# A four-stream graph-attention kernel: one more row by transfer, independent scatters, and a new interleaving of the streams

## The chip, the cores and the metric

The kernel runs on one core of a Trainium2 chip. The metric is the device time of one execution in microseconds (us); times of a kernel are medians of several runs. Engines are called PE (TensorE), DVE (VectorE), ACT (ScalarE), POOL (GpSimd) and SP (SyncE, which here only issues transfers).

## What is computed

The input x has 32 batches of 512 nodes with 256 features, in float32, and one adjacency of 512 x 512. Four layers follow each other. Each normalizes x over the features, takes the positive part h, computes a graph attention and adds the result to x:

```python
h = jnp.maximum(_layernorm(x, axis=-1), 0.0)
x = x + layer(h, adj, W, a)
# an attention: Wh = h @ W; s_i = Wh @ a1; s_j = Wh @ a2
# e = leaky_relu(s_i[:, :, None] + s_j[:, None, :]); masked by adj
# out = softmax(e) @ Wh, then elu or relu
```

Layers 0 and 1 have one head. Layer 2 has four heads of 64 features. Layer 3 is a linear layer to 512 features, an attention without a mask, a second linear layer to 256, and a masked attention, with residuals.

## The kernel before, in words

**An attention without exponentials of a matrix.** With exp taken of each node's two terms alone, exp(leaky_relu(s_i + s_j)) becomes a factor times max(r_i, t_j). So the 512 x 512 weights of a head are one DVE operation per tile of 128 rows: max of a row r, spread over all partitions, with a column t, times the mask (`weights`, L698, its operation at L708). The row r comes in one of two ways. On PE: four transposes of a column that is broadcast to 128 columns fill a PSUM bank (L704, through the helper at L425). By transfers: `rows_out` (L715) makes one small transpose and one store of rows to DRAM, and `spread` (L725) reads one row back to all 128 partitions, 256 KB, into one of three buffers. Layers 0, 1 and the last attention use PE. In layer 2 (L805) heads 1 to 3 use transfers and head 0 uses PE (L822). The products of layer 2 use 32-column tiles of the array, 16 to a bank (`beside`, L419).

**The unmasked attention by sorting.** `sort_attend` (L949) replaces a 512 x 512 product: it spreads one row of terms, counts for each node its place in the order (L969), and POOL scatters the rows of values to DRAM by that place: two orders (halves of the features) of four tiles each, one indirect transfer a tile (L990). SP reads an order back in sequence (L997, L998). DVE and PE make prefix sums from both sides: DVE within a partition (L1008 to L1017), PE across partitions with triangular matrices (`add_up`, L895, called `before` and `after`). SP writes the sums as a table (L1031), and POOL gathers for each node its row of the table (L1039, two buffers). DVE and ACT finish a gathered tile (L1053 to L1058), and `mlp_in` (L1105) turns it by four transposes on PE. Only the last batch uses the direct product (`attend`, L917).

**Four streams and a list scheduler.** Four streams of eight batches each are written as generators. Each `yield` returns a time on a notional clock at which the stream wants to go on (`after_us`, L411, from PE work issued times STRETCH and a given number of us times SLOW). The loop at L1152 always resumes the stream with the earliest time. So the yields set the order in which operations are written down, and nothing else: they are no waits on the chip. That order is each operation's rank. A planner in the kernel's own file (`price`, `jobs_of`, `in_order`) then places all operations on the engines: at each step the operation of the lowest rank whose inputs are ready on its own cost table, with PSUM banks and buffers given out. `LANDING` (L79) and L126 are its assumed times from issue to landing of transfers; `holds` is how long an issue keeps an engine. `arrange` (L376) fixes the order found, engine by engine. Waits on the chip remain real semaphores. SP, POOL, DVE and ACT run strictly in that order, so what stands behind a waiting instruction waits too.

**PSUM banks.** There are eight; each stream has a tag, and a tag's tiles may take one bank of its own or any of four shared ones. `bank` (L430) gives a tile the tag of the stream whose turn it is, and, while other streams haven't started or have ended, their tags in turn.

**Setup.** Weights, adjacency and x are loaded on SP. The mask comes from the adjacency by one DVE comparison (L563), one POOL operation (L564) and 16 transposes on PE with four copies on ACT (L575). Other weights get their attention columns by small products (`project`, L466). The setup is a fifth generator, resumed every 4.0 us of the notional clock from 7.5 on.

Of the kernel before, what the change touches and what calls it, by code (L numbers as in the profile page):

```python
# [78 lines left out]
LANDING = {"sums": 5600.0, "spread": 4400.0, "table": 6500.0, "x": 10000.0, "order": 4100.0, "g": 6300.0, "out": 4500.0}  # L79
# [26 lines left out]
def price(job, outs, ins, in_psum):  # L106
# [15 lines left out]
    if op == "DMACopy":  # L122
        name, _, s = outs[0]
        kind = name.split("_")[0].rstrip("0123456789")
        large = elements(s) * s[0][1] > 5000
        job.took = LANDING.get(kind, 5000.0) if large else 5200.0 if kind == "table" else 2250.0  # L126
        job.holds = (2000.0 if kind == "order" else 1290.0) if e == "Pool" else 600.0 if kind in ("sums", "table") else 400.0
        return
# [28 lines left out]
def jobs_of(instructions, homes):  # L157

    jobs, users, seen, pitch = [], {}, {}, {}
    for place, ins in enumerate(instructions):  # L160
# [6 lines left out]
        for write, access in [(False, a) for a in reads] + [(True, a) for a in writes]:  # L167
# [16 lines left out]
            kept = []  # L184
            for other, wrote, b in seen.get(name, []):
                meets = b[0] < box[1] and box[0] < b[1] and any(c < y and x < d for c, d in b[2] for x, y in box[2])
                if meets and (write or wrote) and other is not job:
                    job.real.add(other)
                    if write and on_chip and box[0] <= b[0] and b[1] <= box[1] and len(box[2]) == 1 and box[2][0][0] <= b[2][0][0] and b[2][-1][1] <= box[2][0][1]:
                        continue  # L190
                kept.append((other, wrote, b))
# [184 lines left out]
def arrange(tc, order):  # L376

    instructions = real_instructions(tc)
    edge = mybir.DependencyInfo(mybir.DependencyClass.NoSync, mybir.DependencyReason.DATA)
    for line in order.values():  # L380
        for a, b in zip(line, line[1:]):
            tc.add_manual_dep(instructions[b], instructions[a].name, edge, reason="arranged")
# [3 lines left out]
def fast(ctx, tc, plan, flag, x, adj, w0, a0, w1, a1, w2, a2, mlp1_w, mlp1_b, mlp2_w, mlp2_b,  # L386
# [10 lines left out]
    LEAD = 75.0  # L397
    SLOW = 1.5
    STRETCH = 2.0
# [27 lines left out]
    active = set()  # L427
    banks = [0]

    def bank():  # L430

        own = [turn[0], *(i for i in range(NS) if i not in active and i != turn[0])]
        banks[0] += 1
        return psum.tile([P, N], FP, tag=f"b{own[banks[0] % len(own)]}", name="b", bufs=8 // NS)
# [125 lines left out]
    def setup():  # L560
# [9 lines left out]
        for j in range(NT):  # L570
            turn[0] = NS - 1 - j % (NS - 1)
            p = bank()
            for t in range(NT):
                transpose(p[:, t * P:(t + 1) * P], own[:, t, j * P:(j + 1) * P], ident)
            nc.scalar.copy(maskT[:, j, :], p)  # L575
        turn[0] = NS - 1
# [70 lines left out]
    def turned(xn, when):  # L647
# [5 lines left out]
        yield after_us(0.6)  # L653
# [9 lines left out]
    def values(hT, w, rs=None):  # L663

        v = work.tile([P, NT, F + 3], FP, tag="v", name="v", bufs=4)
        for t in range(NT):
# [14 lines left out]
            if t + 1 < NT:  # L681
                yield after_us(0)
        yield after_us(0.8)
        return v

    def linear_t(inT, w, bias, name, bufs):
# [3 lines left out]
        for f in range(ft):  # L690
# [4 lines left out]
            yield after_us(0.9 if f == ft - 1 else 0)  # L695
# [47 lines left out]
    def plain(hT, w, rs=None):  # L743
# [3 lines left out]
        yield after_us(3.2)  # L747
# [19 lines left out]
    def layer0(xt, xn, rs, when):  # L767
        v, wt = yield from plain((yield from turned(xn, when)), W0)
        xn, rs = new_xn(), small([NT], "rs")
        for t0 in range(0, NT, 2):  # L770
            r, q = pair(), pair("q")
            for i in range(2):
# [3 lines left out]
                if i == 0:  # L776
                    yield after_us(0)
            add_elu(xt[:, t0:t0 + 2, :], r, q)
            norm(xt, xn, rs, t0, True)
            last, when = when, after_us(6)  # L780
            if t0 == 0:
                yield after_us(0)
# [3 lines left out]
    def layer1(xt, xn, rs, when):  # L786
        v, wt = yield from plain((yield from turned(xn, when)), W1, rs)
        xn, rs = new_xn(), small([NT], "rs")
        for t0 in range(0, NT, 2):
            r = pair()  # L790
            for i in range(2):
                p, rd = averages(v, wt, t0 + i)
                nc.scalar.activation(r[:, i, :], p, AF.Relu, scale=rd)
                if i == 0:
                    yield after_us(0)
# [3 lines left out]
            last, when = when, after_us(5)  # L799
            if t0 == 0:  # L800
                yield after_us(0)
# [3 lines left out]
    def layer2(xt, xn, rs, when):  # L805
        hT = yield from turned(xn, when)
        v = work.tile([P, NT, NH, CH], FP, tag="v", name="v2", bufs=4)
        for t in range(NT):
# [11 lines left out]
            yield after_us(0 if t + 1 < NT else 1)  # L820
        row_d = rows_out(v[:, :, :, D + 2], NH)
        far = [spread(row_d[h, :]) if h else None for h in range(NH)]  # L822
        wts = []

        def begin():
# [4 lines left out]
            return after_us(3.2)  # L830
# [6 lines left out]
        )  # L837
        begin()
        note(v.rearrange("p t h c -> p (t h) c")[:, :, D:])
        yield after_us(3)  # L840
        when = begin()
        for g, parts in enumerate(plan):
# [10 lines left out]
            yield after_us(0.9)  # L853
# [29 lines left out]
            yield after_us(0)  # L883
# [3 lines left out]
        yield after_us(7)  # L887
        return xn, rs, after_us(2)
# [28 lines left out]
    def attend(oT, b):  # L917

        halves, ends = fc_values()
        for c in range(2):  # L920
            for t in range(NT):
                project_half(oT, halves, ends, c, t)
                yield after_us(0)
# [4 lines left out]
        yield after_us(2)  # L928
        ys = []
        for t in range(NT):  # L930
# [10 lines left out]
            yield after_us(0)  # L941
            if t:
                mlp_in(oT, ys[t - 1], t - 1)
                yield after_us(0)
        yield after_us(3)
        mlp_in(oT, ys[-1], NT - 1)
        yield after_us(1)

    def sort_attend(oT, b):  # L949
# [6 lines left out]
        for t in range(NT):  # L956
            project_half(oT, halves, ends, 0, t)
            yield after_us(0)
        project_half(oT, halves, ends, 1, 0)
        yield after_us(0)  # L960
# [3 lines left out]
        yield after_us(7.0)  # L964
# [10 lines left out]
        sort = after_us(6)  # L975
        yield after_us(0)
        for t in range(1, NT):
            project_half(oT, halves, ends, 1, t)
            yield after_us(0)
# [7 lines left out]
        for c in range(2):  # L987
            yield sort
            for t in range(NT):
                nc.gpsimd.indirect_dma_start(  # L990
                    out=orders[c], out_offset=bass.IndirectOffsetOnAxis(ap=at[:, 0, t:t + 1], axis=0),
                    in_=halves[c][:, t, :], in_offset=None,
                )
            flat.append(work.tile([P, NT * 2, C], FP, tag="sums", name="sums", bufs=2))
            u = flat[c].rearrange("p (t k) n -> p t k n", k=2)[:, :, 1, :]
            rows = orders[c].rearrange("(p t) c -> p t c", t=NT)
            nc.sync.dma_start(u, rows)  # L997
            nc.sync.dma_start(flat[c][:, 2, :], rows[:, 0, :])  # L998
            sort = after_us(2)
        places = table[:N, :].rearrange("(p t) (k c n) -> p (t k) c n", t=NT, k=2, c=2)  # L1000
        sort = after_us(11)
        for c in range(2):
# [15 lines left out]
            yield after_us(3)  # L1018
# [14 lines left out]
            sort = after_us(1)  # L1033
        yield after_us(9)
# [12 lines left out]
        landed = after_us(6)  # L1047
        for t in range(NT):
# [13 lines left out]
            landed = after_us(3)  # L1062
            when.append(after_us(4))
# [6 lines left out]
        yield after_us(1.0)  # L1070

    def layer3(xt, xn, when, b):
# [6 lines left out]
        for t0 in range(0, NT, n):  # L1079
            y, q = pair()[:, :n, :], pair("q")[:, :n, :]  # L1080
            for i in range(n):
# [3 lines left out]
                yield after_us(0)  # L1085
# [40 lines left out]
    def batch(b):  # L1126
        if b < NS:
            first_norm(b)
            yield after_us(4)
        else:  # L1130
            yield after_us(4)
        xt, xn, rs = normed.pop(b)
        when = after_us(2)
# [14 lines left out]
    ready = {i: i * LEAD for i in range(NS)}  # L1148
    streams = [stream(i) for i in range(NS)]
    early = setup()  # L1150
    ready[NS] = 7.5
    while ready:  # L1152
        i = min(ready, key=ready.get)
        if i == NS:
            turn[0] = NS - 1
            ready[i] += 4.0
# [5 lines left out]
        active.add(i)  # L1162
        wait = next(streams[i], None)
        if wait is None:
            del ready[i]
            active.remove(i)
# [456 lines left out]
```

## Time and profile before

| | us |
|---|---|
| median of 3 runs | 2814.35 |
| lowest, highest | 2813.93, 2819.74 |
| the profiled execution, own time | 2815.09 |
| its span in the trace | 2812.3 |
| PE busy | 2754.0 |
| DVE busy | 2255.0 |
| ACT busy | 1615.8 |
| POOL busy | 513.7 |

The mean granted clock of PE is 0.996 of full speed. 278.98 MB moved, at a mean of 99 GB/s; the 16 transfer engines are busy for some three tenths. All numbers of the profile are from one execution. The page has busy shares of each engine and of 40 slices of the span, the groups of instructions with their mean durations and what ended the idle time before them, and the transfers. Other views answer for a window: busy time by stage, who waited for whom, and a timeline. In them PE is the matmul row and PEld the weight load, which overlaps it; SPq is SP's queue.

### The profile page before, as it was taken

How to read it: one execution, taken by the hardware profiler on the slowest of the kernel's cores; microseconds unless marked ns; L12 is line 12 of the kernel's file. 1: busy time of each engine (PE TensorE's matmuls, PEld its weight loads, DVE VectorE, ACT ScalarE, POOL GpSimd, SP SyncE). 2: the span in 40 equal slices, each digit the busy share in tenths (PEclk: the TensorE clock that was granted, in tenths of full speed). 3: DMA queues.
4: the chain of work that ended last, by engine and by line, in shares of the span. 5: the costliest groups of instructions: out<-in, count | busy, mean ns of one | idle time of the engine just before them, and what ended most of it. 6: DMA issues, size and time to landing. Idle time of an engine off the chain costs nothing.

```text
span 2812.3 us, 41762 instructions
## 1 busy us (share of the span) xinstructions
PE 2754.0 (98%) x14444; PEld 1969.4 (70%) x14444; DVE 2255.0 (80%) x5834; ACT 1615.8 (57%) x4142; POOL 513.7 (18%) x515
## 2 busy tenths in 40 slices
PE   6999999999999999999999999999999999999987
PEld 5667677767767776767766677776676767777665
DVE  4778887887869879788887888878888788878854
ACT  3446656566556566566665565655655556565544
POOL 0011121122211212122111122011220212211220
PEclk9999999999999999999999999999999999999999
DMA  3023332333323333243331433223332332323320
GB/s 98 23 93 104 107 110 83 103 109 114 109 92 97 119 113 101 71 124 107 117 114 42 121 125 119 93 84 100 119 110 91 106 114 96 109 85 104 109 98 33
DMA packets 197890, 278.98 MB, mean 99 GB/s; under 512 B 17644, under 2 KB 156838, under 8 KB 197672
## 3 DMA queue, kind: packets, MB, share of 16 engines
q1 hardware_dynamic: 167912, 177.95, 20.4%
q0 software_dynamic: 29760, 98.30, 10.4%
q8 instruction: 115, 1.88, 0.3%
q14 instruction: 103, 0.84, 0.1%
HBM read 160.75 MB, written 115.45 MB: 98 GB/s over the span
## 4 chain that ended last, share of the span: by engine, by line
PE 81%; DVE 13%; DMA 3%; ACT 3%; issue 1%; POOL 0%; SPq 0%; ACTq 0%; DVEq 0%; POOLq 0%
PE b L417 62%; PE b L421 10%; PE b L425 9%; DVE w L708 4%; DVE st L624 2%; DMA spread<-row 1%; DVE y L765 1%; DVE y L1094 1%; DMA row<-row 1%; DVE y L758 1%; DVE xn L635 1%; DVE x L759 1%; DMA g<-table,at 0%; DVE q L763 0%; DVE x L797 0%
## 5 line engine op out<-in xcount | busy, mean ns | idle before, releaser
L417 PE MATMUL b<-v,w 128*128 128x257 f32 x3136 | 739.9, 382 | 7.3 <-DVE w L708 7.3
L417 PEld LDWEIGHTS b<-v,w 128*128 128x128 f32 x3136 | 580.9, 191 | 118.8 <-issue 28.6
L417 PE MATMUL b<-WFC,oT 128*128 128x256 f32 (+1 forms) x2048 | 490.4, 380 | 0.0
L417 PEld LDWEIGHTS b<-WFC,oT 128*128 128x128 f32 x2048 | 375.6, 189 | 56.4 <-issue 7.2
L417 PE MATMUL b<-W,hT 128*128 128x259 f32 (+1 forms) x1536 | 389.7, 387 | 1.5 <-ACT hT L645 1.5
L990 POOL DMA_INDIRECT order<-v,at x248 | 269.7, 1087 | 498.3 <-ACT y L852 163.9
L708 DVE SCALAR_TENSOR_TENSOR w<-b,v,maskT 128x512 f32<-128x512 f32 x512 | 353.3, 744 | 3.6 <-PE b L425 3.5
L421 PE MATMUL b<-w,v 128*32 128x512 f32 x3072 | 349.5, 595 | 0.0
L417 PEld LDWEIGHTS b<-W,hT 128*128 128x128 f32 x1536 | 276.0, 191 | 79.3 <-issue 25.3
L1039 POOL DMA_INDIRECT g<-table,at x124 | 125.6, 1013 | 1116.4 <-DVE q L763 251.3
L708 DVE SCALAR_TENSOR_TENSOR w<-spread,v,maskT 128x512 f32<-128x512 f32 x384 | 286.0, 786 | 28.1 <-DMA spread<-row 25.3
L417 PE MATMUL b<-hT,WM 128*128 128x512 f32 x512 | 241.5, 594 | 2.3 <-ACT hT L645 2.2
L421 PEld LDWEIGHTS b<-w,v 128*32 128x32 f32 x3072 | 89.9, 110 | 205.9 <-issue 205.9
L417 PE MATMUL b<-oT,WM 128*128 128x512 f32 x512 | 232.3, 600 | 0.8 <-DVE oT L1112 0.8
L624 DVE BATCH_NORM_STATS2 st<-x 128x6 f32<-128x256 f32 x512 | 195.1, 409 | 2.1
L765 DVE TENSOR_TENSOR y<-q,y 128x512 f32<-128x512 f32 (+1 forms) x194 | 132.3, 682 | 63.9 <-ACT q L764 59.3
L417 PEld LDWEIGHTS b<-oT,WM 128*128 128x128 f32 x512 | 96.6, 191 | 107.0 <-issue 96.6
L425 PEld LDWEIGHTS b<-ident,xn 128*128 128x128 f32 x1024 | 121.3, 141 | 64.3 <-issue 25.4
L425 PE MATMUL b<-ident,xn 128*128 128x128 f32 x1024 | 152.8, 276 | 7.8 <-DVE xn L635 2.7
L645 ACT ACTIVATE hT<-b 128x512 f32<-128x512 f32 x256 | 149.5, 595 | 14.2 <-PE b L425 14.2
L740 DVE RECIPROCAL rden<-b 128x1 f32<-128x1 f32 x388 | 58.4, 158 | 120.3 <-PE b L417 119.6
L915 ACT ACTIVATE v<-b,ends 128x256 f32<-128x256 f32 x256 | 120.0, 470 | 58.3 <-PE b L417 52.4
(154 smaller groups left out, 4230.1 us busy)
## 6 DMA issues: line engine op xcount, KB each, us to landing
table<-sums SPq DMA_DIRECT2D x62, 1032.0 KB
spread<-row SPq DMA_DIRECT2D x127, 256.0 KB
sums<-order SPq DMA_DIRECT2D x62, 516.0 KB
x<-in_x_dram SPq DMA_DIRECT2D x32, 512.0 KB
out_dram<-x SPq DMA_DIRECT2D x62, 256.0 KB
sums<-order SPq DMA_DIRECT2D x62, 129.0 KB
order<-v,at POOLq DMA_INDIRECT x248, 2.7
g<-table,at POOLq DMA_INDIRECT x124, 5.3
```

Source lines behind the costliest of these rows:

```text
L417: nc.tensor.matmul(p, w, x, **flags)
L421: nc.tensor.matmul(p, w, x, tile_position=(0, c), **flags)
L425: nc.tensor.transpose(p, x, i)
L624: nc.vector.bn_stats(st[:, i, :], xt[:, t0 + i, :])
L635: nc.vector.tensor_scalar(xn[:, t0 + i, :], xt[:, t0 + i, :], mv[:, i, 0:1], rp[:, i:i + 1], op0=OP.subtract, op1=OP.mult)
L645: nc.scalar.activation(hT[:, :, t0 * P:(t0 + 2) * P], p.rearrange("p (k n) -> p k n", k=KF), AF.Relu)
L708: nc.vector.scalar_tensor_tensor(wt[:, j, :], r, t_col(j), maskT[:, j, :], op0=OP.max, op1=OP.mult)
L740: nc.vector.reciprocal(r, den)
L765: nc.vector.tensor_tensor(r, q, r, op=OP.add)
L915: nc.scalar.activation(halves[c][:, t, :F], ps[:, :F], AF.Copy, scale=ends[:, t, 0:1])
L990: nc.gpsimd.indirect_dma_start(out=orders[c], out_offset=bass.IndirectOffsetOnAxis(ap=at[:, 0, t:t + 1], axis=0), in_=halves[c][:, t, :], ...
L1039: nc.gpsimd.indirect_dma_start(out=g, out_offset=None, in_=table, in_offset=bass.IndirectOffsetOnAxis(ap=at[:, 1, t:t + 1], axis=0),)
```

## The change

It has five parts.

1. **Head 0 by transfer.** In layer 2 all four rows come by `spread`. The first weights are written down 9.98 notional us after the rows' stores.
2. **Independent scatters.** The four scatters of one order are declared to be free of each other, since they write different rows; both reads of the order get explicit waits on all four. The planner no longer orders them among themselves either. On POOL, `arrange` adds order edges to the next five instructions in place of the next one.
3. **Assumed landing times.** `spread` 4300 ns plus 900 for each later head (4400), gathers 6800 (6300), row stores 2600 and small others 3300 (2250), the first x 5000 (10000), the adjacency 9000 (5000).
4. **Yields.** Nearly all numbers of `after_us` change, LEAD goes from 75.0 to 75.63 with an offset for each stream, SLOW from 1.5 to 1.43, STRETCH from 2.0 to 1.5. The setup is resumed every 1.5 us from 0.35 on.
5. **Banks.** A tile always takes the tag of its own stream; the mask's transposes no longer walk through other streams' tags.

In the order of instructions the changed program has 384 transposes of v on PE where there were 512, 512 products with a spread row and 384 with a row in PSUM (384 and 512), and 159 spread transfers (127). All other counts are the same.

```diff
-LANDING = {"sums": 5600.0, "spread": 4400.0, "table": 6500.0, "x": 10000.0, "order": 4100.0, "g": 6300.0, "out": 4500.0}
+LANDING = {
+    "sums": 5600.0, "spread": 4300.0, "table": 6500.0, "x": 10000.0, "order": 4100.0, "g": 6800.0, "out": 4500.0,
+    "adj": 9000.0,
+}
+SHORT = {"table": 5200.0, "row": 2600.0, "out": 4500.0}
...
-        job.took = LANDING.get(kind, 5000.0) if large else 5200.0 if kind == "table" else 2250.0
+        job.took = LANDING.get(kind, 6000.0) if large else SHORT.get(kind, 3300.0)
+        if kind == "spread":
+            job.took += 900.0 * (ins[0][1] // 512)
+        if kind == "x" and ins[0][1] == 0:
+            job.took = 5000.0
...
+            free = write and name in apart
             for other, wrote, b in seen.get(name, []):
+                if free and wrote and b == box:
+                    kept.append((other, wrote, b))
+                    continue
...
-    for line in order.values():
-        for a, b in zip(line, line[1:]):
-            tc.add_manual_dep(instructions[b], instructions[a].name, edge, reason="arranged")
+    for e, line in order.items():
+        for reach in range(1, 6 if e == "Pool" else 2):
+            for a, b in zip(line, line[reach:]):
+                tc.add_manual_dep(instructions[b], instructions[a].name, edge, reason="arranged")
...
-    LEAD = 75.0
-    SLOW = 1.5
-    STRETCH = 2.0
+    LEAD = 75.63
+    SLOW = 1.43
+    STRETCH = 1.5
...
-        own = [turn[0], *(i for i in range(NS) if i not in active and i != turn[0])]
-        banks[0] += 1
-        return psum.tile([P, N], FP, tag=f"b{own[banks[0] % len(own)]}", name="b", bufs=8 // NS)
+        return psum.tile([P, N], FP, tag=f"b{turn[0]}", name="b", bufs=8 // NS)
...
-        far = [spread(row_d[h, :]) if h else None for h in range(NH)]
+        far = [spread(row_d[h, :]) for h in range(NH)]
...
-            return after_us(3.2)
+            return after_us(1.36)
...
+        yield after_us(9.98)
         begin()
         note(v.rearrange("p t h c -> p (t h) c")[:, :, D:])
-        yield after_us(3)
+        yield after_us(7.5)
...
-        yield after_us(7)
-        return xn, rs, after_us(2)
+        yield after_us(9.4)
+        return xn, rs, after_us(1.32)
...
-        yield after_us(7.0)
+        yield after_us(0.73)
...
-        sort = after_us(6)
-        yield after_us(0)
+        sort = after_us(16.48)
+        yield after_us(7.62)
...
+            placed = []
             for t in range(NT):
-                nc.gpsimd.indirect_dma_start(
+                one = nc.gpsimd.indirect_dma_start(
                     out=orders[c], out_offset=bass.IndirectOffsetOnAxis(ap=at[:, 0, t:t + 1], axis=0),
                     in_=halves[c][:, t, :], in_offset=None,
                 )
+                for other in placed:
+                    tc.declare_no_dep(one.ins, other.ins, reason="rows of one order apart")
+                placed.append(one)
...
-            nc.sync.dma_start(u, rows)
-            nc.sync.dma_start(flat[c][:, 2, :], rows[:, 0, :])
-            sort = after_us(2)
+            landed = mybir.DependencyInfo(mybir.DependencyClass.Sync, mybir.DependencyReason.DATA)
+            for read in (nc.sync.dma_start(u, rows), nc.sync.dma_start(flat[c][:, 2, :], rows[:, 0, :])):
+                for other in placed:
+                    tc.add_manual_dep(read.ins, other.ins.name, landed, reason="rows of four tiles")
+            sort = after_us(1.66)
...
-        sort = after_us(11)
+        sort = after_us(6.05)
...
-        yield after_us(9)
+        yield after_us(4.72)
...
-    ready = {i: i * LEAD for i in range(NS)}
+    ready = {i: i * LEAD + late for i, late in enumerate((0, -2.47, -0.73, -8.03))}
...
-    ready[NS] = 7.5
+    ready[NS] = 0.35
...
-            ready[i] += 4.0
+            ready[i] += 1.5
```

The other yields change in the same way, in every layer: those within a loop over tiles from 0 to between 0.06 and 12.63, those between stages up or down by a few us.

## The prediction

> **What bounds the kernel now.** I read the page's busy shares and slices first, then busy time by stage, then the groups by shape, then who waited for whom on PE and in the queues, and at last the timeline of both ends.
>
> ```profile
> PE 2754.0 (98%) x14444; PEld 1969.4 (70%) x14444; DVE 2255.0 (80%) x5834; ACT 1615.8 (57%) x4142; POOL 513.7 (18%) x515
> PE   6999999999999999999999999999999999999987
> ```
>
> PE is busy all along and short only in the first slice and the last two. The span, 2812.3, is 2754.0 of PE plus 58.3 of idle. The stages (columns: stage, its length, then busy us and instructions of PE, weight loads, DVE, ACT, POOL; granted clock; DMA share; GB/s) say where those 58.3 lie:
>
> ```profile
> 0.00:6.90 6.90, 0.02 (x1) 0.05 (x1) 0.63 (x4) 1.28 (x1) 1.14 (x8) 1.00 0.55 167
> 6.90:17.50 10.60, 2.90 (x12) 2.44 (x12) 5.30 (x6) 0.74 (x2) 2.27 (x3) 1.00 0.86 263
> 17.50:33.50 16.00, 13.75 (x68) 11.46 (x68) 5.13 (x22) 7.56 (x21) 0.84 (x4) 1.00 0.67 181
> 33.50:73.60 40.10, 35.61 (x197) 29.82 (x198) 23.98 (x82) 18.63 (x54) 1.47 (x3) 1.00 0.00 1
> ...
> 1000.00:2000.00 1000.00, 997.07 (x5262) 715.35 (x5261) 830.51 (x2151) 589.47 (x1520) 189.34 (x184) 1.00 0.33 104
> ...
> 2680.00:2700.00 20.00, 16.69 (x59) 9.23 (x56) 11.07 (x31) 12.24 (x29) 7.41 (x8) 0.91 0.38 120
> 2706.00:2718.00 12.00, 7.61 (x22) 4.92 (x21) 9.97 (x19) 2.30 (x7) 0.00 (x0) 0.64 0.25 88
> ...
> 2741.00:2757.00 16.00, 10.55 (x46) 8.25 (x45) 9.73 (x20) 10.44 (x20) 1.59 (x2) 0.79 0.25 83
> ```
>
> The first 214.9 us hold 27.7 of idle, 220 to 2500 only 6.6, the rest 24.7, of which 8.8 follow the last matmul that counts. Between the ends the kernel runs at the rate of PE: only PE work taken out shortens it there. At the ends it is bound by chains that too few streams cover.
>
> **PE work.** Each of 32 batches loses the four transposes that spread head 0's row (L704 by L425).
>
> ```profile
> L425 PE MATMUL b<-ident,v 128*128 128x128 f32 x512 | 83.7, 274 | 1.4 <-ACT v L675 0.8 <-ACT v L674 0.3 <-ACT v L677 0.2
> ```
>
> Its pace is seen in PE's timeline (start, length, line, tiles, count):
>
> ```profile
> 2730.20 0.60 PE L425 MATMUL b<-ident,ends 128*128 128x128 f32 x4
> 2730.70 3.74 PE L417 MATMUL b<-v,w 128*128 128x257 f32 x16
> ```
>
> A mean of 274 ns is latency. In the timeline four such take 0.60 to the end of the last, which itself lasts 0.27, so they start (0.60-0.27)/3 = 110 ns apart; the median start-to-start of this group is 109. 128 x 109 ns = 14.0. The upper bound is the group's busy share, 83.7/512 = 163 ns, or 20.9; the following matmul comes 0.50 after the first of four, so I take 14.0. The order of instructions, before against after, shows nothing else gone from PE: as many matmuls of each other shape, and 193 changes between tile modes in both. **-14.0.**
>
> **What comes in for it.** 32 more transfers of 256 KB on SP's queue, 8.4 MB on 279 (3%), and 32 x 0.35 = 11 us of SP's issue time. Head 0's four products now read SBUF: the two groups of L708 have means of 744 (from PSUM) and 786 ns, so 128 x 42 ns = 5.4 us on DVE, 0.2 points on 80%. Both lie beside PE. On the path is only the row's trip. In the first batch the 16-row transpose is at 73.6, the first product at 80.8, and four take 2.7: some 10 us to the last. I priced PE's new order with start-to-start distances of the trace (109 ns a transpose; 217, 219, 226 and 429 for one pass of 257, 259, 268 and 512 columns, two passes each; 310 a prefix matmul). Between that transpose and the first use of head 0 lie 18.4 to 23.2 us of other PE work, 13.1 in the first batch: hidden. If it were not, 3 us late 32 times is 96 us. Only three spread buffers exist, so the fourth transfer waits on SP for head 0's last product; behind it stand another stream's row, its spread and reads of orders. Bounds for that: 0 (head 3's first use comes 10.4 us or more after head 0's, and its trip and products need 7), and 1 us a batch on PE, nearest to the row "DVE w L708 <- DMA spread<-row: 25.3, 16, 2.9", which costs PE nothing now. I take 0.
>
> **The scatters.** On POOL the eight scatters of a batch alternate now between two orders, and start within 12 us (12.7 to 24.3 after the row's transpose in the first batch), though one holds POOL 0.98.
>
> ```profile
> POOL order L990 <- DMA order<-v,at: 43.6, 48, 2.6
> ```
>
> and in SP's own queue:
>
> ```profile
> SPq L997 <- DMA order<-v,at: 658.9, 54, 27.3
> ```
>
> 43.6 us of waits on landings go. In the new POOL order each order's four stand together, so the first order's last issue moves from the seventh place to the fourth: 6 us earlier or more. SP, which stands 658.9 us at L997 with table writes and spreads behind it, is free earlier. No matmul waits for this now, so it is worth 0 by itself; it pays for the next item.
>
> **The new order in the middle.** Changed yields cost nothing on the chip: they set ranks. They shorten what covers the sort. In PE work, from the ends' row transpose to the first transpose of a gathered tile there are 81.7 to 86.1 us before, 70.6, 70.9, 71.9 and 78.6 after; from the second order's last prefix matmul to that transpose 25 to 31 before, 20.8 to 23.9 after. What the chain needs there is seen where it had no cover, in the drain: prefix to table issue 1.7, table to the gathered product 13.1 to 14.3, product to transposes 4.6: 19.4 to 20.6. It fits by 0.3 to 4. Bounds: 0, and 1 us for three batches in four, 23. It planned with the same holds and longer landings for gathers (6.8 for 6.3; the trace's median is 5.3, largest 7.6), so I take little: **+3.**
>
> **The start.** PE's idle comes from one wait and then many.
>
> ```profile
> PE b L425 <- POOL own L564: 7.7, 1, 7.7
> PE b L417 <- DVE w L708: 5.1, 5, 2.0
> ```
>
> The new DVE order puts x's statistics first (now at 19.4, behind copies that wait for loads), but the mask's first step (L563, at 9.5 now) behind the copy of the four-head weights, which ends at 17.8. Then 1.2 on DVE, 1.9 on POOL: the mask's transposes start at 21.0, not 17.5. Meanwhile x's transposes and two products are done. On DVE the first weights stand behind the tie band, whose mask waits on POOL behind the last weights' load (28.0): 28.4 + 0.9 + 0.6 + four small ones, so 30.6, not 32.8. First averages near 31.4 instead of 33.5: -2. After that PE's order holds stream 1's layer 0 from 29 us of work on (before 39) and stream 2's from 57 (before 82): more to fill with. Idle from 33.5 to 214.9 is 10.9; I halve it, bounds 0 and -9. **-7.**
>
> **The drain.** From 2664 to 2804 PE idles 15.6 us, and the clock is granted at 0.64 to 0.97 in places: weighted by PE's busy time some 7 more. The Trainium skill ("TensorE: Matmul & The Clock Gate", section "Part 1: The HAM clock gate") halves the clock only after an idle window of about 3.4 us. In 2706:2718 no idle stretch exceeds 1.2 us and the clock is 0.64. By the page only the idle could come back; by the row each short stall in a thin stretch costs about half as much again. I go by the row. In the new order batch 30's prefix matmuls alternate with batch 31's first linear layer and batch 29's averages (before, few others stand there: 4.4 idle); the last gathered tile of batch 29 has 33.6 us since its prefix, and needs about 31 (2.9 idle now); batch 30's gathers have covers of 18.6, 24.2 and 25.9 against needs of 19.4, 27 and 29: 4.2 idle for 5.5. Of 22.7 some 13 stay. Bounds -1 and -16. **-9.** The tail of 8.4 us behind the last average is the same code: 0.
>
> **Sum.** 2812.3 - 14.0 + 3 - 7 - 9 = 2785.3 span. The profiled execution took 2815.09, 2.8 beyond its span, and lies 0.7 above the median 2814.35: so 2787.
>
> **Rivals.**
> 1. *Only the transposes count.* The ends stay, as each end's chain is latency whichever stream fills: -14 + 3 gives 2803. For it: the mask is later by 3.5. Against it: two and three streams stand side by side on PE much earlier. 0.23.
> 2. *The ends close almost wholly*: -14 - 12 - 16, and nothing lost between, 2772. Against it: the gathers' cover in the drain is still short. 0.10.
> 3. *The sort falls behind its shorter cover*, at the gathered tiles' transposes (L1108 by L425), in every steady batch. If DVE or SP takes the table 3 us later than in the drain, three batches in four stall 2 to 3 us: 23 x 2.5 = 58 less 30, 2842. It decides from about 1.3 us a batch (30/23). For it: the margin is 0.3 to 4 and SP carries more. Against it: the scatters give 6 us to the front, and DVE has 17% idle. 0.08.
> 4. *It doesn't do what it says*: the scatters still wait, the fourth spread holds SP, and the shift eats most of the gain: 2812. 0.05.
>
> The forecast itself has 0.54. 0.2%, 5.6 us, is about what a measurement can tell from no change: below 2808.7 is faster, above 2820 slower. Faster 0.86, within 0.06, slower 0.08. Range 2771 to 2807: it takes in both rivals on the fast side and the bounds of start and drain, and leaves out the slow two.
>
> **What would show it.** Right: PE near 2733 to 2740 busy; 384 transposes of v; 512 products from spread near 0.75 us; idle under 10 between 220 and 2500; POOL with no waits of order on order; the mask's transposes near 21 and first averages near 31; the clock at 1.00 in more of the drain. Wrong: PE waits for L765 or for spread in each period of 340 us; a first slice as empty as before; SP waiting at L728 for products.

## The result and the profile after

The changed kernel takes 2784.09 us (median of 4 runs, 2782.5 to 2786.01), beside 2814.63 for the kernel before on the same chip: ratio 0.9888, 95% interval 0.9871 to 0.9905. The forecast was 2787. The profiled execution took 2783.36, with a span of 2781.5, 30.8 less than before. The sum came out right, in part by luck: three of its terms are 6 to 8 us off, and the misses partly cancel.

PE's busy time and its row of slices, from the page of the changed kernel:

```profile
PE 2740.6 (99%) x14316; PEld 1953.5 (70%) x14316; DVE 2272.9 (82%) x5834; ACT 1636.1 (59%) x4142; POOL 518.1 (19%) x515
PE   7999999999999999999999999999999999999998
```

PE is busy for 13.4 us less, 0.6 above the forecast's 2733 to 2740, and the last two slices are nearly full. The first slice holds hardly more than before (7 tenths for 6). The stages, columns as in the prediction:

```profile
6.90:17.50 10.60, 6.76 (x24) 4.83 (x23) 4.18 (x14) 3.37 (x10) 0.49 (x3) 1.00 0.85 261
17.50:33.50 16.00, 11.36 (x55) 10.25 (x56) 6.46 (x16) 5.62 (x14) 3.55 (x6) 0.92 0.68 181
33.50:73.60 40.10, 34.91 (x184) 30.30 (x183) 19.32 (x64) 16.66 (x47) 0.00 (x0) 0.86 0.00 1
...
1000.00:2000.00 1000.00, 999.52 (x5248) 709.56 (x5247) 845.64 (x2164) 603.23 (x1527) 195.43 (x191) 1.00 0.34 108
...
2700.00:2720.00 20.00, 17.42 (x85) 14.55 (x83) 8.79 (x19) 9.67 (x20) 5.22 (x6) 1.00 0.51 170
2720.00:2740.00 20.00, 18.03 (x66) 12.23 (x67) 8.82 (x20) 10.34 (x21) 0.00 (x0) 0.91 0.01 4
```

The middle has 0.5 us of idle in 1000 (2.9 before). The drain has its clock back (0.91 in the worse of these two stages, 0.64 before). At the start the column falls from 1.00 to 0.92 and 0.86. But its 1.00 there is no full clock: the records of the clock begin only at 26.4 us before and at 24.2 us after, and where there is no record the column counts 1, and so does the mean of 0.996 for the kernel before. PE's timeline of the kernel before shows the pace there:

```profile
17.54 2.83 PE L425 MATMUL b<-ident,own 128*128 128x128 f32 x12 [7.66 <-POOL own L564]
```

These transposes start 214 ns apart, in the prediction's lines from the drain 109. The changed kernel's start 214 apart too. So both kernels run at half clock up to the first record, with PE busy for 10.2 us before and 11.8 after. What the changed kernel has besides is half clock from 31.0 to 37.9, from 51.5 to 58.4 and from 89.1 to 92.5. Who waited on PE, and in SP's queue:

```profile
PE b L438 <- DVE xn L637: 8.2, 11, 3.8
...
PE b L438 <- POOL own L572: 4.3, 1, 4.3
PE b L438 <- DVE y L771: 3.5, 3, 1.6
```

```profile
SPq L1009 <- DMA order<-v,at: 696.9, 92, 17.7
...
SPq L734 <- DVE w L714: 4.0, 1, 4.0
```

No product of layer 2 stands for a spread's landing. On SP a spread stood once, for 4.0 us, behind a product (L734 issues spreads), so head 0's row came at no cost. The wait of POOL's scatters on each other's landing is gone. SP's waits for the scatters to land (L1009) did not shrink in sum, but SP stands there earlier: the first order's read leaves 6.7 us after the first scatter (median of 31 batches), 12.7 before, and the first gather 43.9 us after it, 48.3 before.

One row needs care, since the experiments turn on it. L771 (L765 before; the line shifts by a few in the variants) is the last DVE step of `elu2_plus1`, and its only result that PE transposes is a finished gathered tile (in `mlp_in`), save in the last batch, where it ends the direct product. So PE's wait on this `y`, anywhere but in the drain, is a wait for gathered rows. The changed kernel has three, all in the drain.

**Where the 30.8 us lie.** I priced each kernel's PE order as the prediction did (start-to-start distances of the trace), scaled it by 1.0042, with which the changed kernel's middle comes out without loss, and compared that with the times in the trace. What a stretch takes beyond its price is lost there, be it idle time or half clock. The start ends at the row transpose (of `ends`) of the fifth sorted batch, the middle at that of the 29th, the drain with the last matmul. "PE work" is the price of the whole order. The first matmul and the tail take 15 us in both.

| | PE work | lost at the start | in the middle | in the drain |
|---|---|---|---|---|
| before | 2735.5 | 32.9 | 2.9 | 25.9 |
| after | 2721.5 | 33.8 | -0.2 | 11.0 |
| difference | -14.0 | +0.9 | -3.1 | -14.9 |
| forecast | -14 | -7 | +3 | -9 |

How a loss is split between start and drain depends on these prices to within some 3 us.

### The profile page after: what moved, and what is told of

It is laid out like the page before. It is cut to its first block, busy times and chain, and to the rows that moved or that the text cites. A ratio compares the mean times of both kernels' runs of the same rounds, so it can differ in the third digit from the quotient of the medians.

```text
span 2781.5 us, 41668 instructions
## 1 busy us (share of the span) xinstructions
PE 2740.6 (99%) x14316; PEld 1953.5 (70%) x14316; DVE 2272.9 (82%) x5834; ACT 1636.1 (59%) x4142; POOL 518.1 (19%) x515
## 4 chain that ended last, share of the span: by engine, by line
PE 94%; DVE 3%; ACT 1%; DMA 1%; issue 0%; SPq 0%
PE b L430 72%; PE b L434 12%; PE b L438 10%; DVE st L630 0%; DMA W<-in_L_gnn_W_dram 0%; DVE xn L637 0%; DVE y L771 0%; DVE y L764 0%; DVE y L1107 0%; DVE w L714 0%; DMA WHA<-in_L_gnn_W_hand_dram 0%; DMA row<-row 0%; ACT q L780 0%; DMA x<-in_x_dram 0%; ACT y L1097 0%
## 5 line engine op out<-in xcount | busy, mean ns | idle before, releaser
L430 PE MATMUL b<-v,w 128*128 128x257 f32 (+1 forms) x3136 | 767.1, 382 | 2.0 <-DVE w L718 1.0
L430 PEld LDWEIGHTS b<-v,w 128*128 128x128 f32 x3136 | 573.5, 191 | 122.8 <-issue 34.2
L430 PE MATMUL b<-W,hT 128*128 128x259 f32 (+1 forms) x1536 | 396.4, 388 | 0.5 <-ACT hT L651 0.5
L714 DVE SCALAR_TENSOR_TENSOR w<-spread,v,maskT 128x512 f32<-128x512 f32 x512 | 373.9, 778 | 13.7 <-PE b L434 13.1
L998 POOL DMA_INDIRECT order<-v,at x248 | 262.4, 1058 | 409.1 <-DVE at L980 147.0
L714 DVE SCALAR_TENSOR_TENSOR w<-b,v,maskT 128x512 f32<-128x512 f32 x384 | 264.5, 741 | 21.9 <-PE b L438 19.7
L1110 POOL TENSOR_TENSOR x<-x,y 128x512 f32<-128x512 f32 x62 | 82.6, 1332 | 1038.2 <-ACT y L1108 1029.0
L1052 POOL DMA_INDIRECT g<-table,at x124 | 134.9, 1088 | 563.1 <-DMA table<-sums 267.3
L771 DVE TENSOR_TENSOR y<-q,y 128x512 f32<-128x512 f32 (+1 forms) x194 | 132.2, 682 | 33.6 <-ACT q L770 33.4
L922 ACT ACTIVATE v<-b,ends 128x256 f32<-128x256 f32 x256 | 120.6, 471 | 64.0 <-PE b L430 51.5
```

The lines of the kernel that those rows point to most:

```text
L430: nc.tensor.matmul(p, w, x, **flags)
L714: nc.vector.scalar_tensor_tensor(wt[:, j, :], r, t_col(j), maskT[:, j, :], op0=OP.max, op1=OP.mult)
L771: nc.vector.tensor_tensor(r, q, r, op=OP.add)
L922: nc.scalar.activation(halves[c][:, t, :F], ps[:, :F], AF.Copy, scale=ends[:, t, 0:1])
L998: one = nc.gpsimd.indirect_dma_start(out=orders[c], out_offset=bass.IndirectOffsetOnAxis(ap=at[:, 0, t:t + 1], axis=0), in_=halves[c][:, t ...
L1052: nc.gpsimd.indirect_dma_start(out=g, out_offset=None, in_=table, in_offset=bass.IndirectOffsetOnAxis(ap=at[:, 1, t:t + 1], axis=0),)
```

## Experiments

**The theory and its rivals.** My theory was that of the prediction's sum: each term stands for itself, so that the transposes alone are worth 14 us, the yields alone the ends, and the scatters about nothing. The first rival was that parts need each other. From the second set of runs on there was another: the planner draws a new plan at each edit, and it is the plan that costs. Each kernel's time is given with its ratio to the kernel before on the same chip; the changed kernel stands at 0.9888, which would be 2786 on the chips of these runs, where the kernel before took 2817.5 to 2817.7. The losses are those of the table above.

**1. The transfer alone**, on the kernel before:

```diff
-        far = [spread(row_d[h, :]) if h else None for h in range(NH)]
+        far = [spread(row_d[h, :]) for h in range(NH)]
```

> The kernel before with one edit: head 0's row by the transfer too. 128 transposes (109.4 ns each) leave TensorE: 14.0 us. Theory A (each cause adds up: the transposes are worth 14.0 and nothing waits for the row): 2800 us, ratio 0.9950, with the start, the middle and the drain losing what they lose in the kernel before (32.9, 2.9 and 25.9 us). Rival (in the order of before, whose first batch of head 0 work stands only a few us behind the row, the trip of the row is not hidden): TensorE waits for the spread in each batch, 1 to 3 us x 32, 2810 to 2840 us.

2880.79 us, ratio 1.0227 (1.0209 to 1.0245): 63 slower with 14.0 us of work less. The rival's mechanism is right, and its size too small. Lost: 56.6 at the start, 65.7 in the middle, 19.2 in the drain. The waits on PE, for the first weights and for the gathered tiles:

```profile
PE b L417 <- DVE w L708: 43.0, 26, 7.8
PE b L425 <- DVE y L765: 17.8, 12, 2.9
```

In this plan 11.0 to 15.9 us of PE work lie over the row's trip, and PE stands for the first weights. Then comes something that I had not priced. Once in each period of four batches (some 341 us) the waits crowd together, and the clock falls to half for 3.4 to 6.8 us behind them.

**2. The yields alone**, on the kernel before: LEAD, SLOW, STRETCH, all numbers of `after_us`, the streams' starts and the setup's ranks as in the change, the wait of 9.98 among them. POOL's longer order edges and the explicit waits of the reads stayed in too; the rest is as before.

> The kernel before with only the new yields, LEAD, SLOW, STRETCH, stream starts and setup ranks; 512 transposes, chained scatters, old landing times, old banks. Theory A (the interleaving alone made the gain beyond the transposes, 14.9 us in the drain, 3.1 in the middle, -0.9 at the start): 2797 us, ratio 0.994. Rival B (the yields were set for independent scatters and revised landing times, and without those the sort chain or the drain stalls): 2815 to 2845 us, with TensorE waiting for the gathered rows or the order's reads in the middle.

2852.35 us, ratio 1.0123 (1.0106 to 1.0139). My theory fell here too. Lost: 47.0, 30.6, 22.2. The rival is right, in its waits too; only its range ended 7 us lower. The longest row on PE is that of the gathered tiles:

```profile
PE b L430 <- DVE y L770: 25.5, 29, 4.8
```

10.7 us of it, in 21 waits, lie in the middle, where the kernel before has 1.5 in 4. The chain of work behind one of them begins at the gather (start, length, what):

```profile
1059.07 7.14 DMA g<-table,at
...
1066.23 0.76 DVE g L1063
...
1068.80 0.61 DVE y L770
...
1069.46 0.77 PE b L430 x5
```

The gather takes 7.1 us from issue to landing, and the tile's transposes stand for it.

**3. The changed kernel with head 0's row by PE again** (the first diff, turned round).

> The changed kernel with head 0's row by TensorE again (512 transposes), all else kept. Theory A (terms add up): +14.0 us, 2798 us. Rival (the new yields hold room for the transfer's trip, which is now left empty of nothing, and the row's arrival was costing something): less than +12 us, 2793 to 2796. If the transposes' place moves the ends too: outside 2793 to 2803.

2820.86 us, ratio 1.001 (1.0001 to 1.0019), some 35 slower than the changed kernel. 14.0 are work; the rest is lost at the start (40.4) and in the middle (16.9); the drain is not worse (9.4). The sum holds for the work and fails for the rest.

**4. Room for the row on the kernel before.** Experiment 1 and one wait more:

```diff
+        yield after_us(9.98)
         begin()
         note(v.rearrange("p t h c -> p (t h) c")[:, :, D:])
```

> The kernel before with head 0's row by the transfer and one wait more: 9.98 us between the rows' transfers and the first head's weights, as the change has it. In TensorE's order 20.0 to 27.3 us of work now lie between the rows' transposes and the first product of head 0 (11.0 to 15.9 with the transfer alone, 18.4 to 23.2 in the changed kernel). Theory A (the transfer alone lost time because the row's trip of some 18 us was not covered; with cover it is worth its 14 us): the waits for L708's weights are gone and the time is 2800 us. Rival (the other waits that appeared with the transfer, for results of DVE and ScalarE in stages far from the row, are from an order that no longer fits its yields, and one wait doesn't mend them): waits for L708 gone, but 2820 to 2850 us.

2860.55 us, ratio 1.0153 (1.0139 to 1.0166). The rival is right in kind; its range ended 10 us lower. The row's waits nearly go, and other stages stall:

```profile
PE b L417 <- ACT hT L645: 17.3, 32, 0.9
...
PE b L417 <- DVE w L708: 4.9, 6, 1.3
```

Lost: 46.8, 46.9, 29.8. L645 is the copy of a transposed h, far from layer 2's rows.

**5. The changed kernel without that wait.**

```diff
-        yield after_us(9.98)
         begin()
```

> The changed kernel without the one wait of 9.98 us between the rows' transfers and the first head's weights. TensorE's order then has 11.4, 16.8, 17.2 and 13.8 us of work over the row's trip in place of 18.4 to 23.2. Theory A (that wait is what hides the trip): TensorE waits for the spread's weights in the middle, 1 to 3 us a batch, and the time is 2825 to 2850 us. Rival (the trip is hidden by the work of the other streams wherever the wait stands): 2784 to 2790 us.

2955.39 us, ratio 1.0492 (1.0478 to 1.0507). Theory A has the right sign; the size, some 170 us, is about three times what I expected, 145.1 in the middle alone. In this plan DVE stands for the spread's landing, and PE behind it, also in other streams' work:

```profile
DVE w L714 <- DMA spread<-row: 51.1, 9, 7.5
```

```profile
PE b L430 <- DVE w L714: 32.8, 23, 1.8
PE b L434 <- DVE y L874: 21.4, 7, 3.1
PE b L438 <- ACT y L1096: 18.6, 7, 2.7
PE b L438 <- DVE y L771: 17.2, 10, 2.6
```

Experiments 1, 4 and 5 together show: without the wait the trip is not hidden, and with it nearly so. The 18 to 23 us over the row are made by this one wait among the new yields, not by the transfer.

**6. Transfer and yields together**, on the kernel before: experiments 1 and 2 in one; chained scatters, old landing times and old banks.

> The kernel before with the transfer and the new yields together, without the three other parts: scatters chained, old landing times, old choice of PSUM banks. Theory A (the pair is the change; each of the two alone lost time because it needs the other, and the three other parts are worth a few us at most): 2784 to 2792 us. Rival B (independent scatters and the revised landing times are what lets the sort's shorter cover hold, and the banks what lets the start hold): 2800 to 2840 us, with waits for the gathered rows in the middle or a start that loses over 40 us.

2815.94 us, ratio 0.9998 (0.9989 to 1.0007). Rival B holds, by the second of its signs: the start loses over 40. Lost: 42.7, 12.7, 21.7. Gathered tiles hardly stop PE in the middle (2.8 us at L770). So the pair alone gains nothing, 31 us short of the whole change.

**7. The scatters chained, and the planner told so.**

```diff
-            free = write and name in apart
+            free = False
...
-                for other in placed:
-                    tc.declare_no_dep(one.ins, other.ins, reason="rows of one order apart")
```

> The changed kernel with each order's four scatters chained again; the rest kept. In the changed kernel the eight scatters of a sorted batch take some 10 us, 1.3 us apart; chained they took 13 to 14. The cover from the last prefix product to the first use of a gathered row becomes 19.9 to 22.7 us (20.7 to 23.9 before the edit). Theory A (the chain of the sort has slack in the middle, so the scatters are worth little): within 4 us of the changed kernel, 2784 to 2788. Rival (my prediction's claim that independent scatters pay for the shorter cover): TensorE waits for gathered rows, 0.5 to 1.5 us a batch in 24 batches, 2796 to 2820.

2838.83 us, ratio 1.0085 (1.0071 to 1.0099). The rival is right in sign and too small (40.8 are lost in the middle), and it names only a part of the waits. In the middle PE stands 11.6 us for gathered tiles, at their transposes (L771) and at the step behind those (`oT` of L1123), and 7.5 for `oT` of L700, which is another stage. The chain of work between 1299 and 1310 shows how a late sort gets there (start, length, what):

```profile
1299.90 0.41 DVE sums L1026
1300.31 0.18 SPq L1042
...
1300.54 0.02 SPq L734
...
1300.58 6.42 DMA spread<-row
...
1307.03 1.63 DVE w L714
```

One stream's table write (L1042) stands at the head of SP's queue until DVE has its sums; behind it stands another stream's spread (L734), which lands 6.4 us later, and only then come that stream's weights. This is one place of several. The chain reaches `oT` of L700 at 1309.62, and PE stands for it.

**8. The scatters chained on the chip, but not in the plan.** Only the last two removed lines of experiment 7; the planner goes on as if they were free.

> The changed kernel in which the planner still counts an order's four scatters as independent, but the program doesn't declare them so: on the chip each waits for the one before. TensorE's planned order stays that of the changed kernel almost line for line. Theory A (the 55 us that chained scatters cost together with a new plan come from the scatters themselves: the order is read some 4 us later, the table is written later, SP stands on that write and a spread behind it is late): 2820 to 2845 us. Rival B (they come mostly from the new plan): 2785 to 2800 us.

2827.5 us, ratio 1.0031 (1.0023 to 1.004). Theory A. On every engine each operation stands in the place that it has in the changed kernel, up to buffer numbers. So this is no other plan, and the 40 us are the scatters' own, in this order of POOL. First POOL, then PE:

```profile
POOL order L998 <- DMA order<-v,at: 193.8, 98, 3.7
```

```profile
PE b L430 <- ACT parts L907: 19.4, 20, 2.6
```

From the first to the last start of a batch's eight scatters it takes 21.4 us (median of 31 batches), 10.1 in the changed kernel, 11.9 in the kernel before, where scatters alternate between the two orders, and 11.7 in experiment 7, which alternates again. PE waits at the prefix sums (`parts`), the first step that needs the order, and hardly at the gathered tiles (1.8 us in the middle). The order of POOL matters to the size: it puts an order's four scatters together, which pays only if they are free. So the 40 us are the price of chaining them in this order; chained in turns, as before, they take only 1.6 to 1.8 us longer than free, and what that alone would cost was not measured apart from a new plan.

**9. The setup's ranks of before**, on the changed kernel.

```diff
-    ready[NS] = 0.35
+    ready[NS] = 7.5
...
-            ready[i] += 1.5
+            ready[i] += 4.0
```

> The changed kernel with the setup's ranks of before (7.5 and a step of 4.0 in place of 0.35 and 1.5); the order from the fifth batch on is the same. Theory A (the start lost 33.8 us where I forecast some 26 because the early setup puts copies and band operations in front of stream 0's first relus and the first weights; TensorE stands 4.5 us at 49.7 to 53.5 for a normalisation whose relus start only at 48.9): the start loses 4 to 5 us less, 2779 to 2780 us, and the wait for the first normalised values at 50 us is gone. Rival (the start is bounded by the inputs' transfers and by four streams that share one chain of DVE and ScalarE work, so that the order of the setup matters little): within 1.5 us of 2784.

2779.32 us, ratio 0.9865 (0.9847 to 0.9882), with a span of 2777.4. Theory A. The start loses 26.9, 6.9 less than the changed kernel's; the middle 0.5, the drain 13.3. ACT's timeline shows the cause, first in the changed kernel, then here:

```profile
48.21 0.47 ACT L780 ACTIVATE q<-b,rden 128x256 f32<-128x256 f32 x1 [0.65 <-DVE rden L746]
48.67 0.37 ACT L481 COPY wT<-b 128x256 f32<-128x256 f32 x1
48.94 1.57 ACT L781 ACTIVATE y<-b,rden 128x256 f32<-128x256 f32 x4
```

```profile
43.12 0.47 ACT L780 ACTIVATE q<-b,rden 128x256 f32<-128x256 f32 x1
43.49 0.47 ACT L781 ACTIVATE y<-b,rden 128x256 f32<-128x256 f32 x1
```

With the early setup all four relus of stream 0's layer 0 (L781) stand behind the setup's copies (L481) until 48.94, though the first three of their exponentials were done by 45.95; so the next normalization is late, and PE idles 3.84 us up to 53.54. Here each relu follows its exponential. Between 33.5 and 214.9 PE idles 5.8 us (8.5 in the changed kernel) and is busy for 3.4 at half clock (12.0). The version beats the kernel before clearly. Against the changed kernel its span is 4.1 lower, while the intervals of the two ratios overlap.

**10 and 11. Two nudges of the changed kernel**, which take no work away: one assumed landing 0.1 us higher, and the wait behind the rows 1 us longer.

```diff
-"order": 4100.0
+"order": 4200.0
```

> The changed kernel with one assumed landing time 0.1 us higher (the read of an order, 4.1 to 4.2 us). It changes nothing that the chip executes but the places of instructions in each engine's order. Theory A (the plan is smooth in such numbers: nearby plans cost nearly the same): within 4 us of the changed kernel's 2784. Rival B (each plan is a draw, so that undoing a part mainly costs because the plan is drawn anew): over 8 us from it, most likely slower, 2792 to 2830.

2785.81 us, ratio 0.9885 (0.9867 to 0.9903): the changed kernel's time. Smooth.

```diff
-        yield after_us(9.98)
+        yield after_us(10.98)
```

> The changed kernel with the wait of 9.98 us behind the rows' transfers set to 10.98 us. One us more cover for a trip that is covered already is worth nothing by itself. Theory A (smooth): within 4 us of 2784. Rival B (each plan is a draw): over 8 us from it, most likely slower, 2792 to 2830.

2825.13 us, ratio 1.0024 (1.0015 to 1.0033). Rival B: one notional microsecond at one yield costs some 39, more than the whole change brings. Lost: 46.0, 26.1, 14.1. At 30% of the places in PE's order another kind of operation stands now, and at 54% of DVE's. All counts of instructions are those of the changed kernel, and no wait is large:

```profile
PE b L438 <- DVE y L771: 11.3, 14, 1.7
...
PE b L430 <- DVE w L714: 6.5, 9, 0.8
PE b L430 <- DVE parts L908: 4.8, 8, 0.6
```

DVE stands 39.3 us, in 34 waits, for a gather's landing, where it has no such wait in the changed kernel. The same few results of DVE, gathered tiles first, are late by some tenths of a microsecond in each period of four batches.

**12. The old landing times**, on the changed kernel (the third part of the change undone).

> The changed kernel with the assumed landing times of the kernel before (adjacency at 5.0 us in place of 9.0, spreads 4.4 for every head, small transfers 2.25, gathers 6.3). Theory A (the kernels with the old times and old banks reached their first products with the mask's weights 10 us later, and it is the adjacency's assumed landing that puts work which waits for it in front of other work): the start loses some 10 us more, the middle some us more, 2795 to 2815 us. Rival B (that came from the banks): the start as in the changed kernel, 2784 to 2790 us.

2791.34 us, ratio 0.9905 (0.9887 to 0.9923): between the two ranges, and its interval overlaps that of the changed kernel. Theory A is wrong at the start: that loses 28.6, 5 less than the changed kernel. The middle loses 11.4, the drain 9.2. In the middle PE stands for gathered tiles (8.6 us in 12 waits; none in the changed kernel), whose landing this plan assumes 0.5 us earlier. The first products with the mask's weights were some 10 us late in experiments 2 and 6, which kept the old banks, and not in 7 or 12; so the banks remain as the cause of that, by exclusion, unless they need the old landing times beside them. They were not tried alone.

## Why the prediction was right, and where it was not

**The transposes, -14.0: right.** PE's busy time fell by 13.4, and the priced orders differ by 14.0.

**The row's trip, hidden: right, for a reason that I read but did not credit.** I found 18.4 to 23.2 us of work over it in the new order. Experiments 1, 4 and 5 show that this is what the yield of 9.98 makes. The transfer alone is 63 us slower. My bound, "3 us late 32 times is 96 us", was the right kind of number. The fourth spread on SP: 0 taken, one wait of 4.0 found.

**DVE's 5.4 us for the SBUF operand: not there.** The two groups of products took 639.3 us before and take 638.4 now. DVE's busy time rose by 17.9, of which one group of 128 x 1 products (`both`) has 9.9, at 232 ns for 154; no wait of PE names it.

**The scatters: their time right, "worth 0 by itself" too narrow.** The waits of 43.6 us on POOL were gone, and the first order's read leaves 6.0 us earlier, as I said. That SP's waits at these reads went from 658.9 to 696.9 is no sign against it: SP comes there earlier and stands longer. But in this very plan the independence is worth some 40 us (experiment 8). I had asked what the waits cost under the old yields. What I called "it pays for the next item" is where their worth lies, and it had to be priced as a condition: this plan holds only with it.

**The middle, +3: wrong sign, small.** It is -3.1. The cover of the sort held: between the fifth sorted batch and the 29th no matmul waits for a gathered tile (1.5 us in 4 waits before). Rival 3, at 0.08, failed in this kernel. But its place was well chosen. Most plans near this one stop PE there: in the middle 10.7 us in experiment 2, 9.3 in 1, 10.5 in 5, 8.6 in 12, 5.5 in 7, 3.9 in 11. A late sort also shows where I did not look: at the prefix sums (experiment 8), and through SP's queue at another stream's weights (experiment 7).

**The start, -7: wrong, +0.9.** The mask's transposes came at 19.4 (forecast 21.0), the first averages at 32.5 (31.4), so the first 33 us went about as I read them, though the gain at the first averages is 1.1 and not 2. Between 33.5 and 214.9 PE's idle fell only from 10.9 to 8.5, where I halved it. And I left out the clock: PE is busy there for 12.0 us at half clock, where it was 0 before, which is some 6 us. (The 1.00 that I read up to 26.4 us was no measurement, but both kernels share the half clock up to 24 us.) The step that failed is "more to fill with": I judged PE's order alone, and what PE waited for was ACT, where the earlier setup put its copies ahead of stream 0's relus. With the setup's ranks of before (experiment 9) the idle time there is 5.8, the half of 10.9 that I had forecast, and the start loses 6.0 less than in the kernel before.

**The drain, -9: right in kind, too small, within its bound of -16.** It is -14.9. From the same point to the last matmul, 140 us in both, idle fell from 15.6 to 7.6. That is 8.0 of the 9 that I had taken for idle and clock together. The clock gave the other part: PE was busy for 16.0 us at half clock, now for 3.4, so some 6 us. I had the row of 0.64 and the choice to go by it, against the Trainium skill ("TensorE: Matmul & The Clock Gate", section "Part 1: The HAM clock gate") as I read it, namely that only a wholly idle window halves the clock. The row was right: the clock fell in that stage without an idle window, and came back when the short stalls went. But I let the clock's part shrink in proportion to the idle, and it went almost wholly.

**The sum** came within 3 us because the start's miss of +7.9 stands against -6.1 in the middle and -5.9 in the drain; that is luck. That it was near at all is not: both kernels have plans that fit them. Their middles lose 2.9 and -0.2 us in 24 batches, while ten of the twelve kernels of the experiments lose 11 to 145 there. I read the plan of the changed kernel itself, and found its covers sufficient; that worked. Reading the diff part by part would not have. One slip has no weight: the idle time of the last stretch, given as 24.7, is 24.0 in the trace, and only so do the three stretches add up to 58.3.

**What stays open.** Why the plan of experiment 11, or of 3, loses 2 to 4 us a period is not traced to one instruction. How much of the gain comes from the banks alone was not tried, nor what the chained scatters would cost in a plan made for them. The drain's gain, half of the whole, was not taken apart either: it is all but gone with the old scatters, landing times and banks together (experiment 6 loses 21.7 there) and whole with the old landing times alone (9.2 in experiment 12), so it needs the scatters, the banks or both beside the yields.

## What to carry to other kernels

Where a list scheduler writes the order and PE is 98% busy, an edit's parts may have no worth of their own: undoing one draws a new plan, and the plan can cost more than the part. So read the new order itself, cover by cover, and keep a control that changes only the plan beside each one-part experiment. What an earlier start of one stream's work pushes back in the fixed order of ACT and DVE must be asked before PE's order is credited, and each stall must be priced with the clock that it costs behind it. Before a wait is named harmless, follow its line in the program to what it finishes: here an unassuming `y` was the end of the sort.

## What the runs showed of the hardware

**The clock follows how busy PE was in the window before.** The records of the granted clock change only at steps of 3.41 us. I laid that grid over the 14 traces, and took each window that is recorded at full clock, with PE's busy share in it. After a share under 0.40 the next window was at half clock in 75 of 75 cases; from 0.40 to 0.55 in 19 of 50; from 0.55 up in 3 of 11,238. So a window need not be idle: waits that fill over 60% of it were always enough, and those that fill 45 to 60% in 19 of 50. In the changed kernel PE idles 3.84 us up to 53.54 and has half clock from 51.5 to 58.4; in the kernel before, 2706:2718 had no stall over 1.2 us, but PE was busy for 0.52 of the window from 2705.8 to 2709.2, and half clock follows from 2709.2 to 2719.5.

**The clock before the first record is not full.** The view gives 1.00 up to 26.4 us in the kernel before; the mask's transposes start 214 ns apart there, and 109 apart later.

**Scatters that are free of each other** start 1.3 us apart in the changed kernel, one of them holding POOL for 0.97. Chained on one order they start 2.8 to 3.7 apart (experiment 8).
